# The first batch of a selective-scan kernel: x loaded ahead of the constants, an early table load, halves of the norm in turn, and gates that wait for the first scan's inputs

## The chip, the cores and the metric

The kernel runs on one core of one Trainium2 chip. The metric is the device time of one execution in microseconds (us), lower is better. Engines are named as in the profile: PE is the matrix engine (PEld its weight load), DVE the vector engine, ACT the scalar engine, POOL the GpSimd engine, and SP the engine that issues most of the DMAs. [...]

## The reference

Two layers stand one after the other, on x of shape (4, 512, 32, 32), float32; a group norm stands before each, and its result is added to x. The change touches only the start of layer 0, which is this (L = 1024 tokens, 512 channels, 1024 inner channels, 16 states):

```python
x = x + mamba(group_norm(x))
# mamba:
xn = layer_norm over channels(x) * ln_w + ln_b
xm, z = split(xn @ W_in)
xs = silu(depthwise causal conv of 4 taps(xm) + conv_b)
proj = xs @ W_x                       # 32 columns for dt, 16 for B, 16 for C
dt = softplus(proj[:, :32] @ W_dt + b_dt)
h[t] = exp(dt[t] * A) * h[t-1] + dt[t] * xs[t] * B[t]      # 16 states per channel
y[t] = sum over states of h[t] * C[t]
out = ((y + xs * D_param) * silu(z)) @ W_out
```

Layer 1 is a position attention with two 3x3 convolutions, whose weights the kernel turns into a transformed form (`u_b`, `u_o` in DRAM) while layer 0 runs.

## The kernel before

Layer 0 works batch by batch with channels on the partitions. A batch has eight blocks of 128 inner channels and two halves of 512 tokens. `norms` loads x in four chunks and does both norms. `conv1` projects a block with `W_in` and does the four taps. `params` makes B and C and writes them to DRAM (`bcd`), `delta` makes dt, the product dt*x (`dtx`, on POOL at L710) and its transpose (`pdt` on PE, `dtxt` by ACT). Then each `unit` is one of 16 states for two blocks and one half: ACT makes the decay (L746), DVE does the scan (L798), PE adds up y (L827). For nine states the scan's second input is made on ACT (`sc`, L758) and turned by PE into a PSUM tile `u` (L784). For the seven others (states 1, 3, 5, ... 13) POOL makes it (`dbx`, L773) from a row of B spread over the partitions by a DMA (`bbc`). The product with C is made on POOL (L820), for states 1, 5, 9 and 13 on DVE (L814). `gates` projects z, copies it (L631), takes silu and stores it to DRAM.

The order of all this is not the order of the code. Each helper records steps with an engine, an assumed duration, a priority and what it reads and writes. `Plan.issue` then plays a small model of five engines and writes the instructions down in the order in which the model starts them. A step on a buffer ring takes a slot of it; the PSUM ring `mm`, which `pmu`, `pvar`, `pz`, `pd` and `pdt` share, has two slots. What is written down is a fixed list for each engine. The waits that the built program has come from what each instruction really reads and writes.

Three pieces of the start matter here.

- **Loads.** The first chunk of x is issued by SP (L394) between `W_in` blocks (`winc`, L568), the pieces of the weight transform (`work`, L1073) and its stores (`u_b`, L1113), as the model orders them. Small constants go out on ACT's queue (L287, L303, L310), `wt_sb` and `pb_sb` on POOL's (L213 to L217). Eight completion semaphores are shared by the DMAs of SP and ACT in turn, so in the built program a DMA often waits until the one that had its semaphore before has landed.
- **The weight transform** (`transform`) is a piece of work for one chunk of 3x3 weights: three loads of 192 KB, two scalings on ACT (L1078, L1079), some 12.4 us of additions on POOL (L1086 to L1106), twelve stores. 32 of them fill the gaps of layer 0. Ten have an early priority and stand before the first scan. A transform's loads reuse the previous one's tiles, so they wait for POOL and for its stores.
- **The norm of batch 0** is one chain: statistics on DVE (L410, L411), two small matmuls (L418, L434), a logarithm and an exponential on ACT (L443, L448), means (`pmu`, L381), first scaling on DVE (L503), squares on ACT (L517), variance (`pvar`, L524), logarithm and exponential (L535, L541), second scaling on DVE (L549), weight and bias on ACT (L557). In batch 0 all of its steps have one priority, so the two halves of `pmu` are written alternately, matmul by matmul. The other batches give a small lag to each stage of the chain.

Of the kernel before, what the change touches and what calls it, by code (L numbers as in the profile page):

```python
# [8 lines left out]
F32 = mybir.dt.float32  # L9
AF = mybir.ActivationFunctionType  # L10
# [5 lines left out]
P = 128  # L16
B, C, HH, WW = 4, 512, 32, 32
L = HH * WW
NCC = C // P
DI = 1024  # L20
NDC = DI // P
NS = 16
RK = 32
# [3 lines left out]
PAB = 64  # L27
# [142 lines left out]
def mamba_then_pab_kernel(  # L170
# [25 lines left out]
    nc = tc.nc  # L196
# [4 lines left out]
    dram = ctx.enter_context(tc.tile_pool(name="dram", bufs=1, space=DRAM))  # L201

    gm_sb = cpool.tile([P, P], F32, tag="gmat", name="gm_sb")
    nc.sync.dma_start(gm_sb, gmat)
    ident = cpool.tile([P, P], F32, tag="ident", name="ident")
    make_identity(nc, ident)

    eps = cpool.tile([P, 1], F32, tag="eps", name="eps")
# [1 line left out]
    ones = cpool.tile([P, P], F32, tag="ones", name="ones")  # L210
    nc.vector.memset(ones, 1.0)
    wt_sb = cpool.tile([P, NCC, 2, PAB], F32, tag="wt", name="wt_sb")
    nc.gpsimd.dma_start(wt_sb[:, :, 0, :], w_top.rearrange("(c p) n -> p c n", p=P))  # L213
    nc.gpsimd.dma_start(wt_sb[:, :, 1, :], w_center.rearrange("(c p) n -> p c n", p=P))
    pb_sb = cpool.tile([P, 1], F32, tag="pb", name="pb_sb")
    nc.gpsimd.dma_start(pb_sb[0:PAB], b_top)
    nc.gpsimd.dma_start(pb_sb[PAB:P], b_center)  # L217

    def padded(b, pool, tag):

# [43 lines left out]
    with ExitStack() as l0:  # L264
        wp = l0.enter_context(tc.tile_pool(name="l0w", bufs=1))
        xtp = l0.enter_context(tc.tile_pool(name="l0x", bufs=1))
# [12 lines left out]

        C_ON_DVE = (1, 5, 9, 13)  # L280

        mean_w = wp.tile([P, P], F32, tag="mean_w", name="mean_w")
        nc.vector.memset(mean_w, 1.0 / C)

        def small(src, name, cols):
            t = wp.tile([P, cols], F32, tag=name, name=name)
            nc.scalar.dma_start(t, src)  # L287
            return t

        lnw_sb = small(ln_w, "lnw_sb", NCC)  # L290
        lnb_sb = small(ln_b, "lnb_sb", NCC)
        cw_sb = small(conv_w, "cw_sb", NDC * 4)
        cb_sb = small(conv_b, "cb_sb", NDC)
        bdt_sb = small(b_dt, "bdt_sb", NDC)
        dp_sb = small(d_param, "dp_sb", NDC)
        a_sb = small(a_log, "a_sb", NDC * NS)


        nc.scalar.activation(a_sb, a_sb, AF.Exp)
        nc.vector.tensor_scalar_mul(a_sb, a_sb, -1.0)  # L300

        wx_sb = wp.tile([P, NDC, RK + 2 * NS], F32, tag="wx", name="wx_sb")
        nc.scalar.dma_start(wx_sb, w_x.rearrange("(d p) n -> p d n", p=P))  # L303


        NP = RK + 2 * NS
        wdt_sb = [wp.tile([P, DI], F32, tag=f"wdt{k}", name=f"wdt_sb{k}") for k in range(2)]
        for k in range(2):
            nc.gpsimd.memset(wdt_sb[k], 0.0)
            nc.scalar.dma_start(wdt_sb[k][k * NP : k * NP + RK, :], w_dt)  # L310


        carry_sb = wp.tile([P, 2, NS], F32, tag="carry", name="carry_sb")
# [28 lines left out]
        def buf(ring, shape, name, free=False):  # L342
            if ring is None:
                return Buf(None, lambda: shape)
            if ring in cells:
                y, x = shape[1:3]
                return Buf(
                    ring,
                    lambda: cells[ring].pop(0).rearrange("p (y x o) -> p y x o", y=y, x=x),
                    done=lambda t: cells[ring].append(t.rearrange("p y x o -> p (y x o)")),  # L350
                )
            pool = {"xt": xtp, "mm": mmp, "u": up, "y0": yp, "y1": yp}.get(ring, sp)
            return Buf(
                ring,
                lambda: pool.tile(shape, F32, tag=ring, name=name, bufs=plan.slots[ring]),
                free=free,
            )

        proj = [buf(None, proj_sb[k * NP : (k + 1) * NP], "") for k in range(2)]
        bts = [buf(None, bt_sb[k], "") for k in range(2)]  # L360
        carry = [[buf(None, None, "") for j in range(2)] for s in range(NS)]
        bcds = [buf(None, t, "") for t in bcd]
        szds = [[buf(None, None, "") for d in range(NDC)] for b in range(B)]
# [3 lines left out]
        xts, ready, xs, dts = {}, {}, {}, {}  # L367
        pieces = buf(None, None, "")
        cells, at = {}, 0
# [18 lines left out]
        def norms(b, prio, lag=0.0):  # L388

            t = xts[b] = buf("xt", [P, NCC, L], f"xt_{b}")  # L390
            src = x[b].rearrange("(c p) h w -> p c (h w)", p=P)
            for c in range(NCC):
                step(
                    "SP", 0.3, lambda c=c: nc.sync.dma_start(t()[:, c, :], src[:, c, :]),  # L394
                    [], [t], prio, kb=512,
                )
            spl = {}
# [167 lines left out]
        def load_win(b, k, prio):  # L565
            w = buf("win", [P, NCC, P], f"winc_{b}_{k}")
            step(
                "SP", 0.3, lambda: nc.sync.dma_start(w(), wiv[:, :, k * P : (k + 1) * P]),  # L568
                [], [w], prio, kb=256,
            )  # L570
            return w

        def project(b, k, w, name, hs, prio, p=None, at=0, holds=()):
            t = xts[b]
            return group(
                name,
                [
                    (
                        lambda c=c: w()[:, c, :], lambda c=c: t()[:, c, hs],
                        [w, ready[b][c]],  # L580
                    )
                    for c in range(NCC)
                ],
                prio, hs.stop - hs.start, [t, *holds], p, at,
            )
# [37 lines left out]
        def gates(b, d, prio):  # L623

            w = load_win(b, NDC + d, prio)
            sz = buf("sz", [P, L], f"sz_{b}_{d}")
            for h, hs in enumerate(halves):
                p = project(b, NDC + d, w, f"pz_{b}_{d}_{h}", hs, prio)
                step(
                    "ACT", 0.48,  # L630
                    lambda hs=hs, p=p: nc.scalar.copy(sz()[:, hs], p()),  # L631
                    [p], [sz], prio,
                )
            step(
                "ACT", 0.97, lambda: nc.scalar.activation(sz(), sz(), AF.Silu),
                [], [sz], prio, "silu",
            )
            step(
                "SP", 0.3, lambda: nc.sync.dma_start(szd[b][d // 2][:, d % 2, :], sz()),
                [sz], [szds[b][d]], prio, kb=512,  # L640
            )
# [42 lines left out]
        def delta(b, e, h, prio):  # L684

            pr = proj[b % 2]
            hs = halves[h]
            name = f"{b}_{e}_{h}"
            dt = buf("dt", [P, 2, T], f"dt_{name}")
            for j in range(2):  # L690
                d = 2 * e + j
                wd = wdt_sb[b % 2][:, d * P : (d + 1) * P]
                pd = group(f"pd_{name}_{j}", [(lambda wd=wd: wd, lambda: proj_sb[:, hs], [pr])], prio)
                step(
                    "ACT", 0.58,
                    lambda d=d, j=j, pd=pd: nc.scalar.activation(
                        dt()[:, j], pd(), AF.Identity, bias=bdt_sb[:, d : d + 1]
                    ),
                    [pd], [dt], prio,
                )  # L700
            step(
                "ACT", 0.97, lambda: nc.scalar.activation(dt(), dt(), AF.Softplus),
                [], [dt], prio, "softplus",
            )
            dtx = buf("dtx", [P, 2, T], f"dtx_{name}")
            us = [xs[b, 2 * e + j] for j in range(2)]

            def times():
                for j in range(2):
                    nc.gpsimd.tensor_mul(dtx()[:, j], dt()[:, j], us[j]()[:, hs])  # L710

            step("POOL", 2.37, times, [dt, *us], [dtx], prio)
            dtxt = buf("dtxt", [P, NK, 2, P], f"dtxt_{name}")
            for j in range(2):
                pt = buf("mm", [P, NK, P], f"pdt_{name}_{j}")

                def turn(j=j, pt=pt):
                    for k in range(NK):
                        nc.tensor.transpose(pt()[:, k, :], dtx()[:, j, k * P : (k + 1) * P], ident)

                step("PE", 4 * TR, turn, [dtx], [pt], prio)
                step(
                    "ACT", 0.48, lambda j=j, pt=pt: nc.scalar.copy(dtxt()[:, :, j, :], pt()),
                    [pt], [dtxt], prio,
                )
            dts[b, e, h] = dt, dtx, dtxt

# [190 lines left out]
                    [res], [x1s[b][h]], at, kb=256,  # L918
                )

        xv = [x[b].rearrange("(c p) h w -> p c (h w)", p=P) for b in range(B)]
        wpv = w_proj.rearrange("(d p) n -> p d n", p=P)

        def load_wpr(name, ds, c, prio):
# [199 lines left out]
                conv1(b, d, at + (PRM["q0"] + PRM["qg"] * d if b == 1 else PRM["c0"] + PRM["cg"] * d))  # L1124
            params(b, at + PRM["p0"])

        norms(0, -200)
        for d in range(NDC):
            conv1(0, d, -190 + d)
        params(0, -180)  # L1130
        for k in range(2 * NPC):
            u, src = ((ub, w_bottom), (uo, w_out))[k // NPC]
# [8 lines left out]
        for b in range(B):  # L1141
            at = b * NDC * NS
            for n in range(NDC):
                e, h = divmod(n, NH)
# [24 lines left out]
    with ExitStack() as l1:  # L1169
# [3 lines left out]
        wp = l1.enter_context(tc.tile_pool(name="l1w", bufs=1))  # L1173
# [13 lines left out]
        for name, src in (("b", b_bottom), ("o", b_out)):  # L1187
            t = wp.tile([1, C], F32, tag=f"brow_{name}", name=f"brow_{name}")
# [357 lines left out]
```

## Time and profile before

| | |
|---|---|
| three runs | median 3146.35 us, 3142.82 to 3151.95 |
| the profiled execution | 3149.88 us, its span 3148.1 us |
| mean granted TensorE clock | 0.965 |
| PE, DVE, ACT, POOL busy | 2791.6, 2314.3, 1859.4, 2181.9 us |
| first scan of the kernel starts (DVE L798) | 163.83 us |
| layer 0 ends, about | 2090 us |

The busy times are sums over stages with different limits. Up to the first scan the kernel is one chain with long waits; from there to about 2090 us four engines share a loop; after it the matrix engine is busy nearly all the time. The profiled execution took 3.53 us more than the median; sums from its rows are made against 3149.88 us.

### The profile page before, as it was taken

Reading aid. Unit: us, or ns where it says so; the run is one execution under the profiler, and the core shown is the slowest. Engines: PE = TensorE matmul, PEld = TensorE weight load, DVE = VectorE, ACT = ScalarE, POOL = GpSimd, SP = SyncE. Lnnn points to the kernel's source line nnn. Section 1 sums busy time; section 2 is a strip of 40 time slices with the busy share of each in tenths; the row PEclk is TensorE's granted clock in tenths of the full one; section 3 lists DMA queues with packets and bytes.
Section 4 is the critical chain, followed back from the end, with each engine's and each line's share of the span. In section 5 each row is a group of like instructions: output and inputs, shape, how many; then the busy total and the mean of one; then the engine's idle time right before and its main releaser. Section 6 shows DMA issues by size and latency. Waiting matters only on the chain. (4 is left out here: it accounts for less than half of the span.)

```text
span 3148.1 us, 36186 instructions
## 1 busy us (share of the span) xinstructions
PE 2791.6 (89%) x11576; PEld 1642.3 (52%) x11576; DVE 2314.3 (74%) x3018; ACT 1859.4 (59%) x3198; POOL 2181.9 (69%) x1207
## 2 busy tenths in 40 slices
PE   4988789989889999888899877779999999999998
PEld 2455556656556656566656555444444444444443
DVE  3488999979998988898987888877285365447344
ACT  3499889997789998789998776652030030030000
POOL 8899997899978899978899998763152142224222
PEclk9999999999899999999999989989999999999999
DMA  6667555488645578745567654357268448628816
GB/s 195 194 188 216 152 159 166 142 249 242 208 122 168 173 214 248 227 127 163 162 193 222 212 179 127 118 146 262 92 233 313 175 158 309 254 82 308 318 68 245
DMA packets 406021, 608.41 MB, mean 193 GB/s; under 512 B 47688, under 2 KB 242504, under 8 KB 381256
## 3 DMA queue, kind: packets, MB, share of 16 engines
q1 hardware_dynamic: 396736, 590.52, 59.0%
q10 hardware_dynamic: 8936, 15.31, 1.3%
q8 instruction: 93, 1.52, 0.2%
q14 instruction: 96, 0.79, 0.1%
q0 software_dynamic: 160, 0.26, 0.0%
HBM read 508.99 MB, written 96.99 MB: 192 GB/s over the span
## 5 line engine op out<-in xcount | busy, mean ns | idle before, releaser
L820 POOL TENSOR_TENSOR da<-da,cbc 128x1024 f32<-128x1024 f32 x288 | 680.6, 2367 | 106.2 <-DVE carry_sb L803 54.3
L773 POOL TENSOR_TENSOR dbx<-dtx,bbc 128x1024 f32<-128x1024 f32 x224 | 528.6, 2371 | 24.8 <-DMA bbc<-bcd 10.8
L758 ACT ACTIVATE sc<-dtxt,bt_sb 128x256 f32<-128x256 f32 x1152 | 504.5, 497 | 48.0 <-PE u L784 46.8
L746 ACT ACTIVATE da<-dt,a_sb 128x512 f32<-128x512 f32 x576 | 394.3, 713 | 60.8 <-PE y L827 60.3
L784 PE MATMUL u<-ident,sc 128*128 128x128 f32 x2304 | 353.8, 286 | 72.5 <-DVE da L798 46.5
L798 DVE TENSOR_TENSOR_SCAN da<-da,carry_sb,u 128x512 f32<-128x512 f32 x288 | 356.2, 1263 | 73.6 <-PE u L784 71.1
L798 DVE TENSOR_TENSOR_SCAN da<-da,u 128x512 f32<-128x512 f32 x288 | 349.1, 1212 | 43.6 <-PE u L784 41.0
L827 PE MATMUL y<-ident,da 128*128 128x128 f32 x2304 | 326.4, 287 | 59.8 <-POOL da L820 56.5
L784 PEld LDWEIGHTS u<-ident,sc 128*128 128x128 f32 x2304 | 277.1, 146 | 181.2 <-DVE da L798 50.7
L827 PEld LDWEIGHTS y<-ident,da 128*128 128x128 f32 x2304 | 276.4, 147 | 163.1 <-POOL da L820 122.0
L1383 PE MATMUL m_b<-uw_b,v_b 128*128 128x512 f32 x768 | 336.0, 594 | 10.3 <-DMA uw_b<-u_b 8.6
L746 ACT ACTIVATE u<-dt,a_sb 128x512 f32<-128x512 f32 x448 | 299.0, 682 | 66.9 <-DVE da L798 34.5
L1383 PE MATMUL m_o<-uw_o,v_o 128*128 128x512 f32 x768 | 333.6, 595 | 4.8 <-DVE v_o L1305 4.1
L827 PE MATMUL y<-ident,dbx 128*128 128x128 f32 x1792 | 269.6, 289 | 54.6 <-DVE dbx L814 37.4
L827 PEld LDWEIGHTS y<-ident,dbx 128*128 128x128 f32 x1792 | 214.2, 148 | 124.3 <-DVE dbx L814 45.7
L381 PE MATMUL pxm<-xt,winc 128*128 128x344 f32 (+2 forms) x768 | 246.6, 468 | 21.0 <-ACT xt L557 8.1
L381 PE MATMUL pz<-xt,winc 128*128 128x512 f32 x512 | 246.9, 602 | 7.6 <-DVE xs L610 3.1
L1383 PEld LDWEIGHTS m_b<-uw_b,v_b 128*128 128x128 f32 x768 | 143.5, 190 | 195.9 <-issue 186.4
L820 POOL TENSOR_TENSOR dbx<-dbx,cbc 128x1024 f32<-128x1024 f32 x96 | 227.2, 2367 | 26.7 <-DVE carry_sb L803 13.7
L1383 PEld LDWEIGHTS m_o<-uw_o,v_o 128*128 128x128 f32 x768 | 145.9, 191 | 191.3 <-issue 184.0
L1431 PE MATMUL pat<-y_b,st 128*128 128x512 f32 x512 | 221.7, 593 | 0.1
L610 DVE SCALAR_TENSOR_TENSOR xs<-pxm,cw_sb,xs 128x341 f32<-128x341 f32 (+4 forms) x288 | 163.7, 570 | 56.9 <-ACT xs L601 50.0
(228 smaller groups left out, 4376.4 us busy)
## 6 DMA issues: line engine op xcount, KB each, us to landing
cbc<-bcd SPq DMA_DIRECT2D x512, 256.0 KB, 3.7
uw_b<-u_b SPq DMA_DIRECT2D x96, 1024.0 KB, 4.8
uw_o<-u_o SPq DMA_DIRECT2D x96, 1024.0 KB, 4.9
bbc<-bcd SPq DMA_DIRECT2D x224, 256.0 KB, 3.9
u_b<-work SPq DMA_DIRECT2D x192, 128.0 KB, 2.4
u_o<-work SPq DMA_DIRECT2D x192, 128.0 KB, 2.7
winc<-in_w_in_dram SPq DMA_DIRECT2D x64, 256.0 KB, 3.9
szd<-sz SPq DMA_DIRECT2D x32, 512.0 KB, 4.1
```

Source lines behind the costliest of these rows:

```text
L381: lambda k=k, lhs=lhs, rhs=rhs: nc.tensor.matmul(p()[:, at : at + cols], lhs(), rhs(), start=(k == 0), stop=(k == n - 1)),
L610: nc.vector.scalar_tensor_tensor(u()[:, first:end], p()[:, first - k - at + before : end - k - at + before], cw[k], u()[:, first:end], ALU ...
L746: nc.scalar.activation(t, dt()[:, j], AF.Exp, scale=a_sb[:, at : at + 1])
L758: nc.scalar.activation(sc()[:, k], dtxt()[:, k], AF.Copy, scale=bt()[:, at, s : s + 1])
L773: lambda: nc.gpsimd.tensor_mul(hc(), dtx(), b_bc().to_broadcast([P, 2, T])),
L784: nc.tensor.transpose(u()[:, k * P : (k + 1) * P], sc()[:, k, j, :], ident)
L798: nc.vector.tensor_tensor_scan(ht, *((hc()[:, j], u()) if on_act else (u(), hc()[:, j])), carry_sb[:, j, s : s + 1] if h else 0.0, ALU.mul ...
L820: lambda: nc.gpsimd.tensor_mul(hc(), hc(), c_bc().to_broadcast([P, 2, T])),
L827: nc.tensor.matmul(y[j]()[:, k, :], hc()[:, j, k * P : (k + 1) * P], ident, start=(s == 0 and k == 0), stop=(s == NS - 1 and k == NK - 1), ...
L1383: nc.tensor.matmul(m[q], v[:, q, k, c, :], w[:, c, :], start=(c == 0), stop=(c == NCC - 1 and not extra),)
L1431: nc.tensor.matmul(pt, st[m][:, 2 * P * j + h : 2 * P * (j + 1) : 2], xb[m // 2][:, m % 2, :], start=(m == 0), stop=(m == NMC - 1),)
```

## The change

Five edits, all on the first batch. The four chunks of x are issued at the very start on SP, ahead of everything else, into a tile that `norms(0)` then takes. All constants (`small`, `wx_sb`, `wdt_sb`, `wt_sb`, `pb_sb`, `gm_sb`) go out on SP behind x, instead of on ACT's and POOL's queues; `a_sb` is the first of them. An extra activation, a logarithm of a constant into `spare`, stands in the code behind the exponential of `a_sb`. `norms(0)` gets a lag of 0.01, so that its halves are ordered one after the other. The projections of `gates` of batch 0 read a marker `begun` that is written by the copies to `dtxt` of the first `delta`, so they come no earlier than those in the order.

```diff
-    nc.sync.dma_start(gm_sb, gmat)
...
-    nc.gpsimd.dma_start(wt_sb[:, :, 0, :], w_top.rearrange("(c p) n -> p c n", p=P))
-    nc.gpsimd.dma_start(wt_sb[:, :, 1, :], w_center.rearrange("(c p) n -> p c n", p=P))
...
-    nc.gpsimd.dma_start(pb_sb[0:PAB], b_top)
-    nc.gpsimd.dma_start(pb_sb[PAB:P], b_center)
...
+        xv = [x[b].rearrange("(c p) h w -> p c (h w)", p=P) for b in range(B)]
+        first = xtp.tile([P, NCC, L], F32, tag="xt", name="xt_0")
+        for c in range(NCC):
+            nc.sync.dma_start(first[:, c, :], xv[0][:, c, :])
+        nc.sync.dma_start(gm_sb, gmat)
...
         def small(src, name, cols):
             t = wp.tile([P, cols], F32, tag=name, name=name)
-            nc.scalar.dma_start(t, src)
+            nc.sync.dma_start(t, src)
             return t
+        a_sb = small(a_log, "a_sb", NDC * NS)
         lnw_sb = small(ln_w, "lnw_sb", NCC)
...
-        a_sb = small(a_log, "a_sb", NDC * NS)
         nc.scalar.activation(a_sb, a_sb, AF.Exp)
         nc.vector.tensor_scalar_mul(a_sb, a_sb, -1.0)
+        spare = wp.tile([P, 1], F32, tag="spare", name="spare")
+        nc.scalar.activation(spare, eps, AF.Ln)
...
-        nc.scalar.dma_start(wx_sb, w_x.rearrange("(d p) n -> p d n", p=P))
+        nc.sync.dma_start(wx_sb, w_x.rearrange("(d p) n -> p d n", p=P))
...
-            nc.scalar.dma_start(wdt_sb[k][k * NP : k * NP + RK, :], w_dt)
+            nc.sync.dma_start(wdt_sb[k][k * NP : k * NP + RK, :], w_dt)
+        nc.sync.dma_start(wt_sb[:, :, 0, :], w_top.rearrange("(c p) n -> p c n", p=P))
+        nc.sync.dma_start(wt_sb[:, :, 1, :], w_center.rearrange("(c p) n -> p c n", p=P))
+        nc.sync.dma_start(pb_sb[0:PAB], b_top)
+        nc.sync.dma_start(pb_sb[PAB:P], b_center)
...
+        begun = buf(None, None, "")
...
             t = xts[b] = buf("xt", [P, NCC, L], f"xt_{b}")
-            src = x[b].rearrange("(c p) h w -> p c (h w)", p=P)
+            if not b:
+                t.tile = first
             for c in range(NCC):
                 step(
-                    "SP", 0.3, lambda c=c: nc.sync.dma_start(t()[:, c, :], src[:, c, :]),
+                    "SP", 0.3,
+                    lambda c=c: b and nc.sync.dma_start(t()[:, c, :], xv[b][:, c, :]),
                     [], [t], prio, kb=512,
                 )
...
-        def project(b, k, w, name, hs, prio, p=None, at=0, holds=()):
+        def project(b, k, w, name, hs, prio, p=None, at=0, holds=(), reads=()):
...
-                        [w, ready[b][c]],
+                        [w, ready[b][c], *reads],
...
-                p = project(b, NDC + d, w, f"pz_{b}_{d}_{h}", hs, prio)
+                p = project(
+                    b, NDC + d, w, f"pz_{b}_{d}_{h}", hs, prio, reads=() if b else [begun]
+                )
...
-                    [pt], [dtxt], prio,
+                    [pt], [dtxt] if b + e + h else [dtxt, begun], prio,
...
-        norms(0, -200)
+        norms(0, -200, 0.01)
```

More of the change, by code (lines that the diff above doesn't have):

```diff
@@ L919, in out_proj @@
                 )
-        xv = [x[b].rearrange("(c p) h w -> p c (h w)", p=P) for b in range(B)]
         wpv = w_proj.rearrange("(d p) n -> p d n", p=P)
```

## The prediction, written before the changed kernel was run

> **What bounds the kernel now.** I read the page first. No engine is full over the span, so the start has to be read by itself.
>
> ```profile
> span 3148.1 us, 36186 instructions
> PE 2791.6 (89%) x11576; PEld 1642.3 (52%) x11576; DVE 2314.3 (74%) x3018; ACT 1859.4 (59%) x3198; POOL 2181.9 (69%) x1207
> ```
>
> Next the timeline of SP's queue, 0 to 30 us: the chunks of x leave at 1.17, 7.86, 8.72 and 14.49 us, the last one behind a store of the first weight transform.
>
> ```profile
> 7.86 0.34 SPq L394 DMA_DIRECT2D xt<-in_x_dram  x1
> 8.24 0.43 SPq L1073 DMA_DIRECT2D work<-in_w_bottom_dram  x1
> 8.72 0.48 SPq L394 DMA_DIRECT2D xt<-in_x_dram  x1
> 13.56 0.89 SPq L1113 DMA_DIRECT2D u_b<-work  x2
> 14.49 0.52 SPq L394 DMA_DIRECT2D xt<-in_x_dram  x1
> ```
>
> Then the timeline of all engines, 0 to 60 us (start, duration, engine, line, idle time before and what ended it):
>
> ```profile
> 13.50 0.52 ACT L1078 ACTIVATE work<-work 128x384 f32<-128x384 f32 x1 [3.48 <-DMA work<-in_w_bottom_dram]
> 19.05 1.29 DVE L410 BATCH_NORM_STATS2 bs_l<-xt 128x6 f32<-128x512 f32 x2 [2.78 <-DMA xt<-in_x_dram]
> 22.02 0.59 PE L434 MATMUL pv_l<-gdev_l,gm_sb 128*128 128x4 f32 x2 [0.79 <-DVE gdev_l L255]
> 25.08 0.52 ACT L1079 ACTIVATE work<-work 128x384 f32<-128x384 f32 x1 [0.79 <-DMA work<-in_w_bottom_dram]
> 25.62 1.28 ACT L443 ACT_TABLE_LOAD   x1
> 39.36 5.36 DVE L503 SCALAR_TENSOR_TENSOR xt<-xt,grstd_l,pmu 128x512 f32<-128x512 f32 x8 [7.65 <-PE pmu L381]
> 43.54 6.91 PE L524 MATMUL pvar<-sq,mean_w 128*128 128x512 f32 x14 [3.36 <-DVE xt L503]
> ```
>
> The norm's logarithm had its input at 22.6 us (22.02+0.59). Its table load starts at 25.62, the moment the scaling L1079 of the *second* weight transform is done: ACT's order, not x, ends last there. From 60.3 us PE carries the convolutions. The views around the first scan (POOL, PE, DVE):
>
> ```profile
> 149.86 2.50 POOL L710 TENSOR_TENSOR dtx<-dt,xs 128x512 f32<-128x512 f32 x2 [10.45 <-ACT dt L702]
> 152.44 2.35 POOL L773 TENSOR_TENSOR dbx<-dtx,bbc 128x1024 f32<-128x1024 f32 x1
> 159.79 1.11 PE L719 MATMUL pdt<-ident,dtx 128*128 128x128 f32 x8 [2.24 <-ACT sz L631]
> 163.83 1.22 DVE L798 TENSOR_TENSOR_SCAN da<-da,u 128x512 f32<-128x512 f32 x1 [20.52 <-PE u L784]
> 247.80 2.46 DVE L798 TENSOR_TENSOR_SCAN dbx<-u,carry_sb,dbx 128x512 f32<-128x512 f32 x2 [5.86 <-POOL dbx L773]
> ```
>
> `dtx` is done at 152.4, but `pdt` starts at 159.8 only, because gate projections hold both `mm` slots until ACT copies them. Later DVE waits for POOL: 5.86, 3.32 and 0.98 us at 247.8, 257.2 and 261.8. POOL itself idles 3.0 us between 150 and 262 (1.13+1.21+0.65): this stage is POOL's. After 262 DVE runs almost without gaps.
>
> [...]
>
> **The change, part by part** (the orders are those of the built program).
>
> *x first.* SP issues a DMA each 0.42 us from 0.73 us. The core moved 156 GB/s in its first 5 us and 249 to 291 after; 2.1 MB take 5+(2.1-0.78)/0.27, about 9 to 10 us. Two statistics and an aggregate add 1.5 and the small matmuls 2.0: the logarithm's input is there at about 13 instead of 22.6. This is worth **nothing**: ACT's order still has both scalings of transforms 0 and 1 before L443.
>
> *Constants on SP.* The first tap load of transform 0 becomes SP's 21st DMA, the third its 24th; each waits until the DMA eight before it has landed. The 12th waits for x's last chunk (9), so the 13th (`wx_sb`, 4.6 us to land) leaves at 9.4 and lands at 14; the 21st leaves then, the 24th at 15.3, or 16.4 if `wt_sb` takes the 5.7 us that it took. The six tap loads of the first 30 us needed 2.0 to 5.4, median 4.2 us. L1078 comes at 16.5 (issue at 13.8 by SP's pace alone, 2.7 to land) to 20.6; I take 19.0 against 13.50: **+5.5** (+3.0 to +7.1). POOL's transforms shift with it. Transform 1's scalings came 9.7 and 11.0 us after POOL began transform 0 (14.11), on waits for POOL and its stores, so they shift too, and **the logarithm starts at 31.1, later than before**. POOL has cover for its own shift: it idled 10.45 us before `dtx`. POOL and ACT issue fewer DMAs; POOL was waiting for taps and ACT for constants then, so that gives nothing.
>
> *Logarithm's table early.* The order is: table and logarithm for `spare`, table and exponential for `a_sb`, four scalings, then a table load for L443 again. The early load is overwritten: **0**; the extra 1.28 us lies where ACT sat idle until 6.55.
>
> *Halves in turn.* `pmu` took 8.80 us for 16 passes from 31.38, slow ones first. The first half's eight end at 36.5; four DVE scalings of 0.67 end at 39.2; the second half's passes end at 39.7, and `pvar` starts then instead of at 43.54 (-3.8). A scaling pair of transform 3, among the squares before, moves behind the exponential (L541), where DVE's second scaling (3.4 us to the first whole chunk) hides its 1.0: -0.6. **-4.4** (-2.5 to -5).
>
> *Convolutions.* PE's work is unchanged. Scaling pairs stand two to four ACT steps later in the order, which fits the earlier norm; with POOL late, one pair (ready about 76 on the old scale) holds a tap copy by 1.6: **+0.5** (0 to +2.2).
>
> *Gates behind the first inputs.* `pdt` can run at 152.4: 1.1, two copies 1.1, four `sc` 1.7, a table 1.3 in that order, decay 0.7: first scan at 157.9, **-5.9** for DVE. But POOL's order now has the second half's `dtx` (2.5), the whole of transform 11 (12.3) and one L820 (2.4) ahead of the first `dbx`. It ends at 149.86+2.5+2.5+12.3+2.4+2.4=171.9, not 154.8. DVE does states 0 and 2 by 163.3 and waits 8.6 for state 1; state 4 is done at 182.1 against 178.2. POOL's sum of work up to 262 is unchanged and starts with the same `dtx`: **0** (-3.0, all its idle time, to +3.9, DVE's lag kept).
>
> Sum: +5.5-4.4+0.5+0 = **+1.6**. The profiled execution would go from 3149.88 to 3151.5; the median lies 3.53 below the profiled one, so 3146.35+1.6, about **3148**. From about 300 us on all lists keep their old order, so the shift should last.
>
> **The rivals.** 0.3% is 9.4 us, about what a measurement of this kernel can tell from no change.
> - *Faster.* The taps are not late, since x no longer competes with them later (shift 0), and the first scan's 5.9 is kept, since POOL's fixed order didn't bind: 0-4.4+0.5-5.9 = -9.8, **3136.5**. For it: DVE's 20.5 us wait before the first scan is the longest there. Against: SP's 24 issues, and DVE's waits on POOL at 247.8 to 261.8.
> - *Slower.* The serial waits on landings cost more than each load alone: transform 0 begins 10 us late, and DVE's 3.9 stay: 10-4.4+0.5+3.9 = +10, **3156**. It decides if L1078 comes after 22.9. For it: `cb_sb` took 5.1 for 4 KB. Against: each wait is eight DMAs old.
> - *The change doesn't do what it says.* Shown above for the table and, in effect, for x. If also the halves gained nothing: +6, **3152**.
>
> **How the numbers follow.** The sum's case, with the idle halves of the norm inside it, 0.66 (own range 3141 to 3155: -5 to +9); faster by over 0.3% 0.21; slower by over 0.3% 0.13. The range, 3133 to 3157, goes a little beyond the faster case, whose terms may all reach their ends, and just past the slower one.
>
> **What would show it.** After: the last x statistic done near 10.5; L1078 first near 19; L443's table load still directly behind a L1079, near 31; `pvar` 8.3 us after `pmu` starts instead of 12.2; `pdt` right behind `dtx`; first scan near 159.5 and then a DVE wait of some 8 us for `dbx`; the 262 us point moved by under 5. A L443 before 25 us, or a DVE that doesn't wait for the first `dbx`, proves me wrong.

## The result and the profile after

| | median | ratio to before, 95% interval |
|---|---|---|
| before, 8 runs beside it | 3150.07 us | 1 |
| changed kernel, 8 runs | 3155.39 us (3152.18 to 3160.74) | 1.0021 (1.0011 to 1.0031) |

The change costs 6.6 us (3.5 to 9.8), within the 0.3% forecast as "no change", 7.4 us above the predicted 3148.0. The profiled executions say the same: 3156.55 against 3149.88 us, spans 3154.7 against 3148.1. From the head of the page after:

```profile
PE 2796.3 (89%) x11576; PEld 1645.0 (52%) x11576; DVE 2302.5 (73%) x3018; ACT 1857.3 (59%) x3198; POOL 2179.9 (69%) x1203
```

The computing is the same (PE has as many instructions, and is busy 4.7 us longer; the three others are busy less), so the difference is looked for in the waits. First SP's queue after, 0 to 22 us:

```profile
0.72 1.81 SPq L281 DMA_DIRECT2D xt<-in_x_dram  x4
...
13.88 1.04 SPq L1085 DMA_DIRECT2D work<-in_w_bottom_dram  x2
...
15.49 0.51 SPq L1085 DMA_DIRECT2D work<-in_w_bottom_dram  x1
```

x has left by 2.5 us, but the three loads of transform 0 leave at 13.88 and 15.49 (before: from 2.69 on). The timeline of all engines after, 0 to 62 us, shows who pays:

```profile
12.14 0.59 PE L445 MATMUL pv_l<-gdev_l,gm_sb 128*128 128x4 f32 x2 [0.79 <-DVE gdev_l L250]
19.91 0.52 ACT L1090 ACTIVATE work<-work 128x384 f32<-128x384 f32 x1 [10.16 <-DMA work<-in_w_bottom_dram]
31.40 0.52 ACT L1091 ACTIVATE work<-work 128x384 f32<-128x384 f32 x1 [0.70 <-DMA work<-in_w_bottom_dram]
31.94 1.28 ACT L454 ACT_TABLE_LOAD   x1
46.12 7.92 PE L535 MATMUL pvar<-sq,mean_w 128*128 128x512 f32 x16
```

The logarithm's input is there at 12.7 us instead of 22.6. Its table load stands behind the same scaling as before and starts at 31.94 instead of 25.62: ten microseconds won, and 6.3 lost. The halves give 4.56 of this back (`pvar` starts 8.43 us after `pmu`, which starts at 37.69; before it was 12.16), and the second logarithm, L546, runs at 54.16 against 52.40. At the first scan (POOL, PE and DVE after, 145 to 180 us):

```profile
152.29 4.96 POOL L723 TENSOR_TENSOR dtx<-dt,xs 128x512 f32<-128x512 f32 x4 [5.08 <-ACT dt L715]
153.62 2.35 PE L732 MATMUL pdt<-ident,dtx 128*128 128x128 f32 x8 [2.33 <-POOL dtx L723]
160.56 1.22 DVE L811 TENSOR_TENSOR_SCAN da<-da,u 128x512 f32<-128x512 f32 x1 [14.82 <-PE u L797]
171.86 2.35 POOL L786 TENSOR_TENSOR dbx<-dtx,bbc 128x1024 f32<-128x1024 f32 x1
174.24 1.23 DVE L811 TENSOR_TENSOR_SCAN u<-u,dbx 128x512 f32<-128x512 f32 x1 [4.98 <-POOL dbx L786]
```

`dtx` is 2.4 us late, the first scan 3.3 us early, and then DVE stands 2.88 and 4.98 us for `u` and `dbx`. At 262 us (three `dbx` in a row, 259.45 before) the shift is +3.2 us, at the norm of batch 2 (843 us) +5.9, and from there to the end it stays between 4.8 and 6.6.

The 2.7 us between are made around batch 1's norm, and they have two parts. From 323.6 us of before on DVE's list is the same in both kernels, so its instructions can be set side by side. ACT and DVE, 335 to 358 us, before:

```profile
336.60 1.05 ACT L850 COPY yt<-y 128x512 f32<-128x512 f32 x2
337.91 0.76 DVE L867 SCALAR_TENSOR_TENSOR pyb<-xs,dp_sb,pyb 128x512 f32<-128x512 f32 x1
```

and after:

```profile
340.11 0.69 ACT L759 ACTIVATE u<-dt,a_sb 128x512 f32<-128x512 f32 x1
340.74 0.70 ACT L759 ACTIVATE da<-dt,a_sb 128x512 f32<-128x512 f32 x1
341.35 1.05 ACT L863 COPY yt<-y 128x512 f32<-128x512 f32 x2
342.66 0.76 DVE L880 SCALAR_TENSOR_TENSOR pyb<-xs,dp_sb,pyb 128x512 f32<-128x512 f32 x1 [1.41 <-PE pyb L873]
357.69 2.72 DVE L514 SCALAR_TENSOR_TENSOR xt<-xt,grstd_l,pmu 128x512 f32<-128x512 f32 x4 [0.98 <-PE pmu L390]
```

At the scan just ahead (335.50 before, 338.79 after) the shift is +3.3 us; at the `pyb` line it is +4.75. ACT's list after has two decays ahead of the copies `yt`, which before follow directly, and DVE waits 1.41 us for what PE makes of them. ACT's two lists are the same only from 353 us of before on. The second part comes at the scaling with `pmu`, where the shift is +6.2 (351.45 before). PE, 345 to 358 us, before:

```profile
345.68 0.95 PE L472 MATMUL pv_l<-gnb_l,mean_w 128*128 128x1 f32 x8
347.40 3.60 PE L381 MATMUL pmu<-xt,mw 128*128 128x512 f32 x8
```

and after:

```profile
350.10 1.71 PE L483 MATMUL pv_l<-gnb_l,mean_w 128*128 128x1 f32 x8
353.40 4.25 PE L390 MATMUL pmu<-xt,mw 128*128 128x512 f32 x8
```

The same instructions take 1.71 instead of 0.95 and 4.25 instead of 3.60 us, and 3.30 us instead of 1.72 lie between their starts. The granted clock was 0.50 and 0.55 in the stretches 349 to 352 and 352 to 355 us after. Before it was 1.00 from 346 to 355 us; its dip (0.60) lay at 343 to 346, ahead of these matmuls.

### The profile page after: what moved, and what is told of

It reads as the page before. It is cut to its first block, busy times and chain, and to the rows that moved or that the text cites. A ratio compares the mean times of both kernels' runs of the same rounds, so it can differ in the third digit from the quotient of the medians.

```text
span 3154.7 us, 36179 instructions
## 1 busy us (share of the span) xinstructions
PE 2796.3 (89%) x11576; PEld 1645.0 (52%) x11576; DVE 2302.5 (73%) x3018; ACT 1857.3 (59%) x3198; POOL 2179.9 (69%) x1203
## 5 line engine op out<-in xcount | busy, mean ns | idle before, releaser
L390 PE MATMUL pxm<-xt,winc 128*128 128x345 f32 (+2 forms) x768 | 245.8, 467 | 18.5 <-ACT xt L568 8.1
```

Of the source, the lines that this page charges most:

```text
L390: lambda k=k, lhs=lhs, rhs=rhs: nc.tensor.matmul(p()[:, at : at + cols], lhs(), rhs(), start=(k == 0), stop=(k == n - 1)),
```

## The experiments

Each ran beside the kernel before. The marks are from one profiled execution of each, in us: the start of the norm's logarithm ("log": L443 in the kernels made from before, L454 or L452 in those made from the changed one), of the first `dtx`, and of the first scan. "Shift" is against before at the start of batch 2's norm (842.69). Gain and loss are the ratio times 3150.

| kernel | median | against before (95%) | log | `dtx` | POOL's wait for it | first scan | shift |
|---|---|---|---|---|---|---|---|
| before | | | 26.92 | 149.86 | 10.45 | 163.83 | 0 |
| changed | 3155.39 | +6.6 (3.5 to 9.8) | 33.23 | 152.29 | 5.08 | 160.56 | +5.9 |
| halves_only | 3146.51 | -3.2 (-5.7 to -0.9) | 27.03 | 143.21 | 2.63 | 159.09 | -6.0 |
| gates_only | 3151.85 | +2.8 (-0.3 to 5.7) | 26.76 | 146.82 | 7.37 | 155.77 | -2.0 |
| consts_back | 3152.74 | +3.5 (0.3 to 6.6) | 29.51 | 145.93 | 3.04 | 156.16 | +2.5 |
| no_spare | 3154.51 | +5.4 (2.8 to 7.6) | 32.59 | 151.47 | 5.05 | 159.42 | +4.3 |
| no_begun | 3155.30 | +6.9 (4.4 to 9.4) | 32.50 | 152.38 | 5.14 | 166.94 | +5.9 |
| norm_ahead | 3160.53 | +10.7 (7.2 to 14.2) | 12.32 | 135.41 | 0 | 145.28 | +10.9 |
| norm_ahead_consts | 3158.85 | +7.9 (4.7 to 11.0) | 15.69 | 136.78 | 0 | 145.38 | +10.4 |
| norm_ahead_consts_t9 | 3138.32 | -10.4 (-13.9 to -7.2) | 15.88 | 137.06 | 0 | 147.10 | -9.5 |
| before_t9 | 3149.31 | -0.9 (-4.1 to 2.2) | 26.98 | 150.14 | 22.92 | 166.23 | +0.1 |
| after_t9 | 3152.10 | +2.5 (-0.6 to 5.7) | 33.07 | 150.95 | 16.77 | 158.71 | +1.0 |
| best_no_gates | 3144.04 | -5.4 (-8.2 to -2.5) | 17.07 | 137.86 | 0 | 147.96 | -5.9 |
| best_t8 | 3137.43 | -12.6 (-16.7 to -8.5) | 15.36 | 131.25 | 7.31 | 140.23 | -17.2 |

One caution for the marks: a single execution lies up to 5 us from its kernel's median (consts_back 3147.53 against 3152.74). Part of that comes before `dtx`. In the profiles of before, changed, no_spare and no_begun the eight `pd` matmuls ahead of the first softplus took 5.68 to 5.95 us, with the granted clock at 0.50 to 0.55 from 142 to 148 us; in those of gates_only, halves_only and consts_back they took 3.89 us, with the clock at 1.00 in that stretch (in halves_only they run from 138.06, and it read 0.84 from 136 to 142). PE in the changed kernel and in gates_only:

```profile
145.34 5.95 PE L390 MATMUL pd<-proj,wdt_sb 128*128 128x512 f32 x8
```

```profile
141.67 3.89 PE L381 MATMUL pd<-proj,wdt_sb 128*128 128x512 f32 x8
```

So about 2 us of a difference in `dtx` between these two sets is the clock's, not an edit's. Verdicts go by the medians.

**halves_only**: before, with the one line of the halves.

```diff
-        norms(0, -200)
+        norms(0, -200, 0.01)
```

> The kernel before, with nothing but the halves of the first norm in turn. In the trace of before POOL stood 10.45 us waiting for the first dtx, so the chain norm, convolutions, softplus set that stage. Theory (a shorter norm is passed on as far as POOL has a wait to give up): the pvar group starts about 8.3 us behind the pmu group instead of 12.2, L535 is about 4.4 us earlier, POOL's wait for dtx falls to about 6, and 4 us of it are left at the 262 us point and at the end: 3146 against 3150 us. In the issue order the planner now puts the second dtx and transform 11 ahead of the first dbx; if POOL's whole work up to 262 us is what counts, this costs nothing. Rival (the late dbx costs DVE more than the norm gives): the first dbx ends near 168 instead of 154.8, and the point at 262 us is at 0 to +4. Rival (taps of the transforms hold the convolutions): 0 to -1.

`pvar` starts 8.92 us behind `pmu`, L535 3.9 us earlier, and the gain at the end is 3.2 us: the theory holds. (POOL's wait for `dtx` fell further than forecast, to 2.63 us; the clock's 2 us are in that.) The issue order of this kernel has the second `dtx` and transform 11 ahead of the first `dbx` (164.22 instead of 152.44), with no gate moved. That order comes with this one edit, and it cost nothing that shows.

**gates_only**: before, with `begun` as in the change.

> The kernel before, with nothing but the first batch's gate projections and gates put behind the first scan's inputs. Theory (POOL sets this stage): DVE's first scan is 5 to 6 us earlier than 163.83, but POOL's work is the same and starts at the same time (dtx at 149.86), so the 262 us point and the end move by less than 1 us. Rival (DVE sets the stage; here the first dbx stays ahead of transform 11, so DVE has nothing to wait for): -4 to -6 us at 262 us and at the end, 3145 against 3150. Rival (the gates' work, pushed back, collides later with PE and ACT): +2 to +5.

Here the first `dbx` stays ahead of transform 11 (done at 153.3), so nothing holds DVE, and the first scan is 5.0 us early beyond what `dtx` is early. POOL at its first `dbx` (the other marks are in the table):

```profile
150.92 2.35 POOL L773 TENSOR_TENSOR dbx<-dtx,bbc 128x1024 f32<-128x1024 f32 x1 [1.60 <-DMA cbc<-bcd]
```

At 262 us it is 2.6 us ahead, no more than its `dtx` is (3.0), and at the end it is not faster. DVE's 5 us are worth nothing while POOL's sum is the same: the DVE rival falls. Whether the edit costs up to 2.8 us later isn't settled by an interval that touches 0.

**consts_back**: the changed kernel with the old queues for constants.

```diff
-            nc.sync.dma_start(t, src)
+            nc.scalar.dma_start(t, src)
...
-            nc.sync.dma_start(wdt_sb[k][k * NP : k * NP + RK, :], w_dt)
+            nc.scalar.dma_start(wdt_sb[k][k * NP : k * NP + RK, :], w_dt)
-        nc.sync.dma_start(wt_sb[:, :, 0, :], w_top.rearrange("(c p) n -> p c n", p=P))
+        nc.gpsimd.dma_start(wt_sb[:, :, 0, :], w_top.rearrange("(c p) n -> p c n", p=P))
```

> The changed kernel, with the constants' transfers back on ACT's and POOL's queues; x is still first on SP's. Theory (the constants ahead of winc and work on SP start transform 0 late, and ACT's queue passes that to the norm's logarithm): the first transfers of work are issued near 5 us instead of 13.88, L1090 runs at 13.5 to 15 instead of 19.91, L454's table load at 25 to 27 instead of 31.94, dtx about 5.5 us earlier than 152.29, and the end is 4 to 6 us below the changed kernel: 3150 against 3155.4. Rival (the stage is held by something else, the loss of the changed kernel is made after 340 us): the early marks move as said, and the end by less than 1.5 us.

The end is 3.1 us below the changed kernel (ratios 1.0011 and 1.0021, their intervals overlap). But the marks miss: L1090 comes at 17.66, not at 13.5 to 15 (all engines, 0 to 31 us):

```profile
13.19 0.37 SPq L1085 DMA_DIRECT2D work<-in_w_bottom_dram  x1
17.66 0.52 ACT L1090 ACTIVATE work<-work 128x384 f32<-128x384 f32 x1 [9.58 <-DMA work<-in_w_bottom_dram]
29.08 0.52 ACT L1091 ACTIVATE work<-work 128x384 f32<-128x384 f32 x1 [0.60 <-DMA work<-in_w_bottom_dram]
29.51 0.25 ACT L454 ACTIVATE gdev_l<-pv_l,eps 128x4 f32<-128x4 f32 x1
```

With all constants but `gm_sb` off SP, transform 0 is still 4.2 us late (17.66 against 13.50); the constants' place on SP adds 2.25 (19.91). The 4.2 us are not x's alone. Its first two loads do leave at 7.58 us, behind x, instead of 2.69. But L1090 starts when the third has landed, which left at 13.19, and SP had issued nothing for the 3.2 us before it (from 9.96), 1.3 of them after x's last chunk was there (its statistics start at 11.85). Such a wait can be for a constant on ACT's queue: in before, SP stood 1.4 us for `cb_sb`, ahead of the `winc` at 7.24. How the 4.2 us divide between x and such waits is not shown. And here ACT's order has the logarithm's early table behind the exponential's, so L454 follows L1091 with no load between them.

**no_spare**: the changed kernel without the logarithm on `spare`.

> The changed kernel without the logarithm on the spare column. Theory: one table load and 0.2 us less in the first 3 us of ACT, where it waits for a_log's transfer anyway: 0, within 1 us of the changed kernel (3155). As a second record of almost the same instructions it also tells whether the 3.4 us that the changed kernel lost between 340 and 393 us come again: if they come from where TensorE's granted clock dipped (0.77 in the stretch 350 to 360 us, where before had 1.00), the same stretches should show the same dips and the shift against before should again be near +3 at 262 us and near +6 at 393 us. Rival (they are this one execution's): +3 at 262 us and +2 to +4 at 393 us, with the clock's dips elsewhere.

0.9 us by the medians: no effect of the early table can be told. The loss at batch 1's norm came again, DVE's wait for `pyb` with 1.42 us as well as the slow matmuls: `pv_l` 1.70 us and `pmu` 4.15, 3.31 us apart, the clock at 0.53 and 0.50 from 346 to 352 us, and a shift of +1.9 at 262 and +5.0 at 390 us. In no_begun and consts_back too 3.3 us lie between the two, in halves_only 1.72 as in before. So the slow matmuls are no accident of one execution.

**no_begun**: the changed kernel without the gates' wait.

```diff
-                    reads=() if b else [begun]
+                    reads=()
...
-                    [pt], [dtxt] if b + e + h else [dtxt, begun], prio,
+                    [pt], [dtxt], prio,
```

> The changed kernel without the gates' wait (the gate projections may again stand ahead of the first scan's inputs). Theory (POOL sets the stage): DVE's first scan is 5 to 6 us later than 160.56, but the first dbx is still behind transform 11 and ends near 172 to 174, so the 262 us point stays within 1 us; the end is 0 to 3 us below the changed kernel (3152 to 3155), since the gates alone in the kernel before read +2.6. Rival (DVE's earlier scans are worth something): 3 to 6 us above the changed kernel.

The first scan is 6.4 us later and the median is the same (3155.30 and 3155.39): in the changed kernel the gates' wait is worth nothing.

This kernel also separates the two parts of the loss around batch 1's norm. From 314 us on its ACT list is that of before, and there is no wait at `pyb`; the clock is 0.55 from 340 to 350 us and 0.76 from 350 to 360, and the matmuls are slow (`pv_l` 1.71, `pmu` 4.87 us). From the scan at 335.50 to the scaling with `pmu` the shift goes from +2.9 to +5.6 us. In halves_only ACT's list is that of before too, and the clock is 1.00 at these matmuls (343 to 349 us); over the same stretch the shift stays within 0.3 us (-3.2 to -3.0). So the slow matmuls alone cost 2.7 us here. In the changed kernel they cost 1.5 us, behind the 1.5 that ACT's order had cost already.

**norm_ahead**: the changed kernel; `normed` is written by the small exponential (L459).

```diff
-            step("ACT", 0.83, scales, [], [ends, mids], prio, fill=True)
+            step("ACT", 0.83, scales, [normed], [ends, mids], prio, fill=True)
```

> The changed kernel; the transforms' scalings on ACT are planned only behind the first norm's second small table step, so that the logarithm no longer stands behind L1090 and L1091, which wait for work. Theory (x first is worth nothing in the changed kernel only because ACT's queue holds the logarithm): L454 runs at 13 to 15 instead of 33.23, the pmu group at 18 to 20 instead of 37.69, L546 near 36 instead of 54.16, dtx at 133 to 137 instead of 152.29 with 9 transforms ahead of it instead of 10. POOL had only 5.08 us of wait for dtx to give up and starts at the same time, so 4 to 8 us of this are left at 262 us and at the end: 3148 against 3155. Rival (the chain of the norm sets everything): -15 to -18 us, 3138. Rival (the convolutions then wait for winc and taps): the marks move until L546, dtx and the end by less than 2 us.

x first now pays (ACT, 8 to 20 us):

```profile
9.32 1.28 ACT L454 ACT_TABLE_LOAD   x1
12.32 0.26 ACT L454 ACTIVATE gdev_l<-pv_l,eps 128x4 f32<-128x4 f32 x1 [1.72 <-PE pv_l L445]
```

The logarithm is 21 us earlier than in the changed kernel and `dtx` 17; still the kernel reads some 4 us slower than that one (their intervals overlap). POOL's list has the first `dbx`, then transforms 10 and 11, and only then the second `dbx`. DVE's timeline shows that wait:

```profile
174.58 1.22 DVE L811 TENSOR_TENSOR_SCAN dbx<-u,dbx 128x512 f32<-128x512 f32 x1 [17.36 <-POOL dbx L786]
```

At 262 us 3.6 us of the 17 are left against the changed kernel. By 634 us they are lost again, and it is at +10.9 by 843 us. The engines' lists differ from those of before until about 803 us here, and no run separates a cause. Forecast were 4 to 8 us at both points: nearly met at 262 us, wrong in sign at the end, as were the rivals.

**norm_ahead_consts**: the same with consts_back's edit.

> As norm_ahead, and the constants back on ACT's and POOL's queues. There the planner's order leaves the logarithm's table in place, so its load falls out of the chain. Theory: L454 at 12.5 to 14.5 with no table load directly ahead of it, transform 0 on POOL at 17 to 18 instead of 20.5; as POOL sets the stage, 2 to 4 us better than norm_ahead at 262 us and at the end: 3145. Rival (the constants' place is worth nothing once the norm is ahead): the same as norm_ahead within 1.5 us.

POOL starts 1.2 us earlier, and the end moves by 1.7 us, inside both intervals: no effect of the constants' place can be told here. The forecast 3145 rested on a gain of norm_ahead that did not come.

**norm_ahead_consts_t9**: one transform fewer at the urgent place.

```diff
-o0=14.48, og=5.23, dl=9.01, t0=10, tg=21.42)
+o0=14.48, og=5.23, dl=9.01, t0=9, tg=21.42)
```

> As norm_ahead_consts, and one transform fewer at the front (nine instead of ten at the urgent place), so that the first two dbx stand ahead of transform 10 on POOL and only one transform stands among the first states. Theory (POOL sets the stage, at 12.4 us a transform): the 262 us point is 8 to 12 us ahead of norm_ahead_consts; the transform left for later costs up to 12.4 us again where POOL has no slack, so the end is 0 to 10 us below norm_ahead_consts: 3140. Rival (POOL is as short later): the 262 us point moves and the end does not, 3145.

POOL, 137 to 147 us:

```profile
137.06 2.50 POOL L723 TENSOR_TENSOR dtx<-dt,xs 128x512 f32<-128x512 f32 x2
139.63 2.35 POOL L786 TENSOR_TENSOR dbx<-dtx,bbc 128x1024 f32<-128x1024 f32 x1
142.15 2.35 POOL L786 TENSOR_TENSOR dbx<-dtx,bbc 128x1024 f32<-128x1024 f32 x1 [0.17 <-DMA bbc<-bcd]
144.75 1.81 POOL L1098 TENSOR_TENSOR work<-work 128x768 f32<-128x768 f32 x1 [0.26 <-ACT work L1090]
```

Two `dbx` stand ahead of one transform instead of one ahead of two. The 262 us point is 11.2 us ahead of norm_ahead_consts, and the end 20 us. It beats both kernels: 0.9967 (0.9956 to 0.9977) of before. The 262 us point moves by about one transform (12.4 us), which POOL has not yet done there; this was forecast. For the end the theory had allowed 10. There no price for it shows; the 9 us by which the end moved further are made between 262 and 843 us, and their cause is open.

**before_t9** and **after_t9**: `t0=9` alone, in each of the two kernels.

> The kernel before with one transform fewer at the urgent place (nine instead of ten), nothing else. It tells whether norm_ahead_consts_t9 won by the norm or by this number alone. Theory (the two need each other): in before the chain to the first dtx is late, POOL already waits 10.45 us for it, and a transform less only makes this wait some 12 us longer; dtx stays at 147 to 150, the 262 us point within 2 us of before, and the transform that is left for later costs 0 to 10 us: 3150 to 3160. Rival (the number alone does it): -8 to -12 us at 262 us and at the end, 3139.

> The changed kernel with nine transforms instead of ten at the urgent place, nothing else. Theory (as before_t9): POOL's wait for dtx grows from 5.08 to 15 to 18 us, dtx stays near 152, the 262 us point within 3 us of the changed kernel's 262.64 (the first dbx is 12 us earlier, which is worth at most that), the end 0 to 8 us above the changed kernel: 3155 to 3163. Rival (the number alone does it): 3143 to 3147, 8 to 12 us below the changed kernel.

Neither gains what the pair does: -0.9 and +2.5 against before (both ends lie a little under their forecast ranges, both 262 us points a little outside theirs). POOL, before_t9 and then after_t9:

```profile
150.14 2.50 POOL L710 TENSOR_TENSOR dtx<-dt,xs 128x512 f32<-128x512 f32 x2 [22.92 <-ACT dt L702]
```

```profile
150.95 2.50 POOL L723 TENSOR_TENSOR dtx<-dt,xs 128x512 f32<-128x512 f32 x2 [16.77 <-ACT dt L715]
```

POOL's freed 12 us turn into wait for `dtx`, which stays where it was. Against before, the early norm alone and the shorter list alone give nothing; together they give 10.4 us. At the 262 us point it reads the same: +1.2 (norm_ahead_consts), +2.9 and -0.3 (these two), -10.1 (the pair). Beyond that point the pair's lists differ from those of before until about 2008 us, so what else the new order did to the end is not separated.

**best_no_gates**: norm_ahead_consts_t9 without the gates' wait.

> norm_ahead_consts_t9 without the gates' wait. Theory (the wait of the gates is worth nothing, as in no_begun and gates_only): within 3 us of norm_ahead_consts_t9, 3136 to 3141. Rival (with the POOL work shortened, DVE now sets the stage, and the gates' 5 to 6 us come back): 3142 to 3145.

The rival's number came: 3144.04, 5 us worse (ratios 0.9983 and 0.9967; their intervals just overlap). Its mechanism did not: the first scan starts at 147.96 us, only 0.9 later than in norm_ahead_consts_t9, and as far behind `dtx` (10.1 and 10.0 us). The difference grows to 2.7 us by the 262 us point and 3.7 by 843. Why is open, and with the overlap it is not certain that the gates' wait is worth anything here.

**best_t8**: norm_ahead_consts_t9 with `t0=8`.

> norm_ahead_consts_t9 with eight transforms instead of nine at the urgent place. Theory (nine is where POOL's transforms and the chain to dtx end together, 137 us): POOL now waits some 10 to 13 us for dtx, which stays at 135 to 137; nothing is gained at 262 us beyond 3 us, and the transform is still to be done: the end is 0 to 10 us above norm_ahead_consts_t9, 3138 to 3148. Rival (every transform taken from the front is 10 us of the end): 3128.

`dtx` came 6 us earlier still (131.25, POOL waiting 7.31 for it); how much of this is the granted clock's at the `pd` matmuls is not shown for this pair. The shift reached -17.5 us by 1123 us. Some 4 us are given back where layer 0 ends, from -15.3 at 1993 us to -11.6 at 2047 us on the time of before. There POOL does this kernel's last transform, which ends at 2013.6 us on its own time; in norm_ahead_consts_t9 it ends at 1919.5. That the late transform costs these 4 us is likely by its place, not shown. The median, 3137.43, is that of t9 within the interval. My theory's front half was wrong, its forecast for the end was missed by 0.6 us, and the rival's 10 us did not come.

## Why the prediction was right, and where its steps were wrong

The forecast of no change holds. Half of the 7.4 us between 3148.0 and 3155.39 is the base: the three runs of before had a median of 3146.35, the eight beside the change, which include those three, 3150.07. The profiled pair moved by 6.67 us against a sum of 1.6. So part of the agreement is luck: 3155.39 lies just above the central case's own range (3141 to 3155), and 1.6 us under the top of the whole. The signs that the prediction named for the first 262 us all came (L1090 at 19.91, its logarithm's table load at 31.94, the shift at +3.2); what it missed comes after. By its steps:

- **What bounds**, right: ACT's order held the logarithm and POOL the stage behind it. ACT kept to its list: L454 had its input at 12.7 us, and its table load came at 31.94, directly behind L1091 (31.40, 0.52 long); in norm_ahead, where the list has it ahead of the scalings, L454 runs at 12.32.
- **"x first: nothing"**: right as a gain. As a cost it was put at nothing, and that isn't shown: with the constants off SP's queue 4.2 of the 6.4 us that transform 0 is late remain, and they are x's in a part that is open (consts_back).
- **"Constants on SP +5.5"**: L1090 came +6.41 late; as a total 0.9 above the forecast and inside its range. As a cause the constants' place on SP is worth 2.25 us by the marks (3.1 at the end), under half of it. The waits on the DMA eight before are in SP's queue after: `bdt_sb`, its 11th, stood 1.5 us and left at 7.77, as x's third chunk landed; `dp_sb`, the 12th, stood 1.0 us for x again.
- **"Logarithm's table early: 0"**: right. After the loads at 0.72 (for `spare`) and 2.23 (the exponential) a third came at 31.94, 1.28 us each; no_spare reads no difference.
- **"Halves in turn -4.4"**: 4.56 in the changed kernel, 3.2 (0.9 to 5.7) at the end alone.
- **"Convolutions +0.5"**: L546 to `dtx` took 0.67 us longer. `dtx` is at +2.43, where the sum had +1.6.
- **"Gates: 0"**: right in the changed kernel: first scan at -5.7 against `dtx`, waits of 7.86 us against 8.6 forecast, and no_begun the same as the change. Its reason for the late first `dbx` was wrong: halves_only has that order without gates, gates_only doesn't.
- **"The shift should last"**, the step that failed: +3.2 at 262 us became +5.9 at 843 us. Its reason, that all lists keep their old order from about 300 us on, holds for POOL, DVE and PE (from 303, 324 and 325 us), not for ACT (from 353): two decays ahead of `yt` cost 1.5 us. Another 1.5 came with TensorE's granted clock on batch 1's small norm matmuls (0.50 and 0.55 from 349 to 355 us), which the prediction did not consider; no_begun and halves_only separate the two. Before, the dip (0.60, 343 to 346 us) lay ahead of the same matmuls, in halves_only too (0.56, 340 to 343). What sets its time is open.

Of the rivals, the faster one fell with gates_only and no_begun: earlier scans alone gave nothing, as they would where POOL binds. The slower one gave 3156, close to what came, but by a mechanism that didn't happen: L1090 was 6.4 us late, not 10.

## What to carry to other kernels

Here a load moved ahead was worth nothing while a list behind it did not let it through (ACT's: input at 12.7 us, table load at 31.94), and what it was moved past came later (L1090 by 6.4 us): follow both before sizing it. Where two chains meet (here the norm's through `dtx`, and POOL's transforms), shortening one gives the other's slack and no more; the gain came only when both were shortened. Attribute by single edits, and compare the lists of every engine before calling a stretch unchanged: two of my reasons (for the late first `dbx`, and for a shift that lasts) were wrong under a sum that was nearly right. A number that comes out as forecast, as in best_no_gates, does not show its mechanism; the marks do.

## What the runs showed that I had not expected

The granted clock moved the marks by as much as the edits did: the eight `pd` matmuls took 3.89 or 5.95 us, and batch 1's pair of groups 1.72 or 3.30 us from start to start. In stretches of 3 us the clock read 0.50 (349 to 352 us after) or 1.00 (355 to 358), and values between, such as 0.55 and 0.81. Both dips near batch 1's norm came behind a stretch in which PE had little to do (busy 0.67 of 3 us before, 1.12 of 3 after). In consts_back and norm_ahead_consts_t9 L454 (at 29.51 and 15.88 us) had no table load directly ahead of it: with the order exponential first and logarithm second the 1.28 us load fell away, which the changed kernel's early load did not save.
